# A two-layer convolution and state-space kernel: the first stage's 3×3 convolutions divided between TensorE and VectorE, with its normalising and copying on ScalarE

## The chip, the cores and the metric

The kernel runs on one core of one Trainium2 chip. The metric is the device time of one execution in microseconds (us). Of several executions the median counts. The profile is that of one further execution, and it carries its own time.

## What is computed

There are two layers over an image batch `x` of 4 images, 128 channels, 64×64 pixels, all in float32. The change lies in the first half of layer 0, which runs once for each image. Cut to that half, the reference is:

```python
x  = group_norm(x)                                  # 32 groups of 4 channels
feat = gelu(dwconv2d(x, conv1_w) + conv1_b)         # depthwise 3x3, 'SAME'
ca   = sigmoid(relu(feat.mean((2, 3)) @ ca1_w.T) @ ca2_w.T)
feat = gelu(dwconv2d(feat * ca, conv2_w) + conv2_b) # depthwise 3x3 again
scores = sigmoid(einsum('bchw,oc->bohw', feat, head_w) + head_b)
final  = 0.7 * scores + 0.3 * sigmoid(10 * var(x over channels))
idx    = argsort(-mean of final over 4x4 patches)   # 256 patches per image
x1  = x with its patches in the order idx, transposed to tokens, + pe
x1n = layer_norm(x1) * norm_g + norm_b
```

`x1n` goes through a Mamba-like block (projection, a scan over 4096 tokens, projection back). Layer 1 follows: a selective scan and a spectral convolution over the same 4 × 4096 tokens. None of that code is changed.

## The kernel before

`conv_attn_hybrid` calls four stages one after the other: `layer0_front` (the code above), `layer0_scan`, `spectral_weights` and `layer1`. `layer0_front` stores its result for each image with `dma_start(xnt[b], xn)` (L259), and `layer0_scan` starts from it. In `layer0_front` a scheduler orders each engine's instructions. It puts in the semaphore waits, also those of an engine for itself, and may interleave independent work. Each engine then executes its list strictly in that order. (`layer0_scan` and what follows have an order written out by hand.)

One image, `for b in range(NB)`, goes like this. Channels are on the 128 partitions.

1. **Group norm.** The image `xs` is loaded. Eight `bn_stats` (L111) and a `bn_aggr` on VectorE, two tiny matmuls (L119, L124) and a GpSimd power (L127) give mean and scale. VectorE writes the normalised image into `xg`, a 66×66 tile with a border of zeros (L129). The `bn_stats` of the next image are interleaved into this image's first convolution.
2. **Patches.** Four VectorE copies (L134) bring the image into patch order (`xp1`). TensorE transposes it to tokens in eight groups of four transposes (L149). For each group VectorE adds `pe` into `x1` (L151) and takes `bn_stats` of both (L153, L154). Per half image, 32 `bn_aggr` follow (L156, L157).
3. **Layer norm of the tokens.** VectorE makes `ve` (L160), GpSimd raises it to the power −0.5 (`r1`, L161), and 32 VectorE instructions subtract the mean and multiply by `r1`, in place in `x1` (L166).
4. **First convolution.** A depthwise 3×3 convolution as nine matmuls, one for each tap: the stationary matrix is diagonal (`d1`, the tap's weights on the diagonal), the moving one is a shifted window of `xg`. `conv` (L90 to L99) sums nine matmuls of 128×128 by 128×512 into one PSUM tile `ps`; eight such tiles cover an image. ScalarE takes each through Gelu into `f1` with a running sum (L176).
5. **Channel attention.** The sums become `mean` (L181, L182), two small matmuls and a Sigmoid give `ca` (L190), and VectorE scales the nine diagonals by it (`d2b`, L192).
6. **Second convolution.** The same on `f1` with `d2b`; Gelu into `f2` in patch order (L196).
7. **Ranking.** 32 small matmuls make the scores (`sc`, L206; the first 16 read the tiles 0 to 3 of `f2`, the next 16, in four groups of four, the tiles 4 to 7), then a short VectorE chain compares all patches and makes a permutation matrix `perm`.
8. **Reordering.** Eight PSUM tiles of four matmuls `x1 × perm` each (L255). VectorE evicts each with `* norm_g + norm_b` into `xn`, with a step of 16 elements between neighbours in the output (L258).

The pool `pm` has four PSUM tiles; transposes, convolutions and reordering share them. Each float32 matmul shows as two records in the trace, so an image's convolution has 8 × 9 × 2 = 144 of them.

Of the kernel before, what the change touches and what calls it, by code (L numbers as in the profile page):

```python
# [8 lines left out]
F32 = mybir.dt.float32  # L9
AF = mybir.ActivationFunctionType  # L10
ALU = mybir.AluOpType
# [3 lines left out]

NB = 4
L = 4096


@with_exitstack  # L20
def layer0_front(ctx: ExitStack, tc, ident, half, w, x, xnt, perm_t):
# [4 lines left out]
    nc = tc.nc  # L26
    cp = ctx.enter_context(tc.tile_pool(name="a_c", bufs=1))
    xp = ctx.enter_context(tc.tile_pool(name="a_x", bufs=1))
    sm = ctx.enter_context(tc.tile_pool(name="a_sm", bufs=2))
# [3 lines left out]
    def load(name, shape, src):  # L33
        t = cp.tile(shape, F32, name=name)
        nc.sync.dma_start(t, src)
        return t

    def column(name, src):
        return load(name, [src.shape[0], 1], src.unsqueeze(1))

    w1 = load("w1", [128, 9], w["conv1_w"])
    w2 = load("w2", [128, 9], w["conv2_w"])
    b1, b2 = column("b1", w["conv1_b"]), column("b2", w["conv2_b"])
# [3 lines left out]
    ng, nb = column("ng", w["norm_g"]), column("nb", w["norm_b"])  # L47
    pe = load("pe", [128, 2, 16, 128], w["pe"].rearrange("(h p) (o c) -> p h o c", p=128, o=16))


    d1 = cp.tile([128, 9, 128], F32, name="d1")
    d2 = cp.tile([128, 9, 128], F32, name="d2")
    for tap in range(9):
        nc.vector.tensor_scalar(d1[:, tap, :], ident, w1[:, tap : tap + 1], None, ALU.mult)
        nc.vector.tensor_scalar(d2[:, tap, :], ident, w2[:, tap : tap + 1], None, ALU.mult)

# [24 lines left out]
    def bordered(name):  # L81

        t = xp.tile([128, 66, 66], F32, tag=name, name=name)
        nc.vector.memset(t[:, 0, :], 0.0)
        nc.vector.memset(t[:, 65, :], 0.0)
        nc.vector.memset(t[:, 1:65, 0:1], 0.0)
        nc.vector.memset(t[:, 1:65, 65:66], 0.0)
        return t, t[:, 1:65, 1:65]

    def conv(img, diag, h, oy):  # L90

        ps = pm.tile([128, 8, 64], F32, tag="mm", name="conv")
        for tap in range(9):
            dy, dx = divmod(tap, 3)
            y0 = 32 * h + oy + dy
            nc.tensor.matmul(  # L96
                ps, diag[:, tap, :], img[:, y0 : y0 + 29 : 4, dx : dx + 64], start=tap == 0, stop=tap == 8
            )
        return ps  # L99

    def by_patch(t, oy):

        return t.rearrange("c (py px oy ox) -> c oy py px ox", px=16, oy=4, ox=4)[:, oy]

    for b in range(NB):

        xs = xp.tile([128, L], F32, tag="xs", name="xs")
        nc.sync.dma_start(xs, x[b])
# [19 lines left out]
        xg, inside = bordered("xg")  # L128
        nc.vector.tensor_scalar(  # L129
            inside, xs.rearrange("c (y x) -> c y x", x=64), gm, rs, ALU.subtract, ALU.mult  # L130
        )
        xp1 = xp.tile([128, L], F32, tag="patches", name="xp1")
        for oy in range(4):
            nc.vector.tensor_copy(  # L134
                by_patch(xp1, oy), inside[:, oy::4, :].rearrange("c py (px ox) -> c py px ox", ox=4)
            )


        x1 = xp.tile([128, 2, 16, 128], F32, tag="x1", name="x1")
# [3 lines left out]
        mv1 = sm.tile([128, 2, 16, 2], F32, tag="mv1", name="mv1")  # L143
        patches = xp1.rearrange("c (h p o) -> c h o p", h=2, o=16)
        for h in range(2):
# [12 lines left out]
        r1 = sm.tile([128, 2, 16], F32, tag="r1", name="r1")  # L158
# [2 lines left out]
        nc.gpsimd.tensor_tensor(  # L161
            r1.rearrange("p h o -> p (h o)"), ve.rearrange("p h o -> p (h o)"), half[:, :32], ALU.pow
        )
        for h in range(2):
            for o in range(16):
                nc.vector.tensor_scalar(  # L166
                    x1[:, h, o, :], x1[:, h, o, :], mv1[:, h, o, 0:1], r1[:, h, o : o + 1],
                    ALU.subtract, ALU.mult,
                )


        f1, inside1 = bordered("f1")
        sums = sm.tile([128, 8], F32, tag="sums", name="sums")
        for i in range(8):
            h, oy = divmod(i, 4)
            nc.scalar.activation(  # L176
                inside1[:, 32 * h + oy : 32 * h + oy + 29 : 4, :], conv(xg, d1, h, oy), AF.Gelu, bias=b1,
                accum_out=sums[:, i : i + 1],
            )
        mean = sm.tile([128, 1], F32, tag="mean", name="mean")  # L180
        nc.vector.tensor_reduce(mean, sums, AX, ALU.add)  # L181
        nc.vector.tensor_scalar(mean, mean, 1.0 / L, None, ALU.mult)  # L182
        hid = ps1.tile([32, 1], F32, tag="one", name="hid")
# [4 lines left out]
        nc.tensor.matmul(cap, ca2, hs, start=True, stop=True)  # L188
        ca = sm.tile([128, 1], F32, tag="ca", name="ca")
        nc.scalar.activation(ca, cap, AF.Sigmoid)  # L190
        d2b = xp.tile([128, 9, 128], F32, tag="d2b", name="d2b")
        nc.vector.tensor_scalar(d2b, d2, ca, None, ALU.mult)  # L192
        f2 = xp.tile([128, L], F32, tag="patches", name="f2")
        for i in range(8):
            h, oy = divmod(i, 4)
            nc.scalar.activation(  # L196
                by_patch(f2, oy)[:, 8 * h : 8 * h + 8],
                conv(f1, d2b, h, oy).rearrange("c py (px ox) -> c py px ox", ox=4), AF.Gelu, bias=b2,
            )


# [2 lines left out]
        for h in range(2):  # L204
            for o in range(16):
                nc.tensor.matmul(  # L206
                    sc[:, h, o : o + 1], fpatch[:, h, o, :], head,
                    start=True, stop=True,
# [38 lines left out]

        xn = xp.tile([128, 3 + L], F32, tag="xn", name="xn")
        nc.vector.memset(xn[:, 0:3], 0.0)
        ranked = xn[:, 3:].rearrange("c (r o) -> c o r", o=16)  # L250
        for o in range(0, 16, 2):
            ps = pm.tile([128, 2, 256], F32, tag="mm", name="ranked")
            for i in range(2):
                for h in range(2):
                    nc.tensor.matmul(  # L255
                        ps[:, i, :], x1[:, h, o + i, :], perm[:, h, :], start=h == 0, stop=h == 1
                    )
            nc.vector.tensor_scalar(ranked[:, o : o + 2, :], ps, ng, nb, ALU.mult, ALU.add)  # L258
        nc.sync.dma_start(xnt[b], xn)  # L259


# [6 lines left out]
def layer0_scan(ctx: ExitStack, tc, ident, w, x, xnt, perm_t, x2):  # L268
# [141 lines left out]
    def put_back(b, om):  # L410

        for h in range(2):
            xs = sm.tile([128, 8, 4, 64], F32, tag="xs", name="xs")
            cols = bass.ts(h, L // 2)
            nc.sync.dma_start(xs.rearrange("c py oy x -> c (py oy x)"), x[b][:, cols])
# [825 lines left out]
@with_exitstack  # L1241
def conv_attn_hybrid(ctx: ExitStack, tc, w, out):
    nc = tc.nc
    const = ctx.enter_context(tc.tile_pool(name="const", bufs=1))
    dram = ctx.enter_context(tc.tile_pool(name="dram", bufs=1, space=DRAM))
    ident = const.tile([128, 128], F32, name="ident")
    make_identity(nc, ident)
    half = const.tile([128, 32], F32, name="half")
    nc.vector.memset(half, -0.5)
    x2 = dram.tile([NB, 128, L], F32, name="x2")  # L1250
    x3 = dram.tile([NB, 128, L], F32, name="x3")
    x = w["x"]
    with tc.tile_pool(name="ordered", bufs=1) as pool:
        xnt = dram.tile([NB, 128, 3 + L], F32, name="xnt")
        perm_t = pool.tile([128, NB, 2, 256], F32, name="perm_t")
        layer0_front(tc, ident, half, w, x, xnt, perm_t)
        layer0_scan(tc, ident, w, x, xnt, perm_t, x2)
    pqd = dram.tile([NK, 2, 128, 4, 128], F32, name="pqd")
    mud = dram.tile([128, 4, 3, 128], F32, name="mud")
    spectral_weights(  # L1260
        tc, w["sigma"], w["M_u"], w["M_phi_plus"], w["M_phi_minus"], w["log_weights"], w["gumbel"], pqd, mud
    )
    layer1(
        tc, ident, half, w["W_in"], w["W_delta"], w["W_B"], w["W_C"], w["W_out"], w["A"], w["phi"], pqd, mud,
        x2, x3, out,
    )
# [48 lines left out]
```

## Time and profile before

| | |
|---|---|
| median of 3 runs | 22132.84 us (22130.33 to 22134.94) |
| the profiled execution | 22129.28 us, its span 22127.6 us |
| end of the first stage's last reordering (L258) in the span | 774.8 us |
| time from one image to the next in the first stage | 187.5 us |
| engine busy time in the span: TensorE, VectorE, ScalarE, GpSimd | 80%, 92%, 71%, 91% |

Engine names in the profile are PE (TensorE), PEld (its weight loads), DVE (VectorE), ACT (ScalarE), POOL (GpSimd) and SP (SyncE, which issues the DMAs). In a timeline or a chain, a row's first number is its start and its second its length, in us from the start of the span. A group's row gives busy time in us and the mean length of one instruction in ns, then the idle time of its engine just before it and what ended that. Consecutive instructions of VectorE or ScalarE overlap a little in the records, so the step from one start to the next is shorter than the length of one.

### The profile page before, as it was taken

What the parts mean: (1) busy time and instruction counts of PE and PEld (TensorE: products, weight loads), DVE (VectorE), ACT (ScalarE), POOL (GpSimd) and SP (SyncE); (2) the same over time, 40 slices, a digit from 0 to 9 for tenths busy, and PEclk for the clock granted to TensorE, in tenths of its full rate; (3) what the DMA queues carried; (4) which work ended last, traced back from release to release, by engine and by line L of the source; (5) the groups of instructions that cost most, each with busy time, mean ns of one, the idle gap of its engine ahead of it and who ended that gap; (6) DMA issues with size and microseconds to landing.
All of it is one profiled execution on the core that took longest, in us unless ns stands there. A gap on an engine that the chain in (4) does not pass through costs nothing.

```text
span 22127.6 us, 292872 instructions
## 1 busy us (share of the span) xinstructions
PE 17758.9 (80%) x99156; PEld 7777.4 (35%) x99156; DVE 20448.7 (92%) x11842; ACT 15725.0 (71%) x28971; POOL 20181.7 (91%) x5932
## 2 busy tenths in 40 slices
PE   8788844474867888886858888869598899999999
PEld 4444421131323333342323333324233344434344
DVE  3588879999999999999999999999999999999993
ACT  0477747777777777777777777777777777777773
POOL 0477759999999999999999999999999999999993
PEclk9899976686988999997979999979699999999999
DMA  0255544464656776675656777757577677777775
GB/s 27 78 139 140 140 136 151 150 198 151 206 186 200 218 222 218 218 220 180 213 173 217 220 219 218 220 179 229 164 225 222 216 233 233 232 230 230 230 226 154
DMA packets 2399971, 4238.15 MB, mean 192 GB/s; under 512 B 778200, under 2 KB 1235968, under 8 KB 2395136
## 3 DMA queue, kind: packets, MB, share of 16 engines
q1 hardware_dynamic: 2398464, 4219.40, 62.0%
q8 instruction: 781, 12.80, 0.2%
q14 instruction: 726, 5.95, 0.1%
HBM read 3600.52 MB, written 617.88 MB: 191 GB/s over the span
## 4 chain that ended last, share of the span: by engine, by line
DVE 49%; POOL 17%; PE 14%; ACT 9%; issue 6%; DMA 4%; SPq 0%; DVEq 0%; POOLq 0%; ACTq 0%
DVE s L1097 43%; POOL v L1085 16%; ACT da L1094 6%; PE conv L1045 6%; DVE states L493 3%; PE conv L96 2%; DMA yd<-ye 2%; PE yp L1114 2%; DVE p L497 2%; PE fin L989 1%; ACT f L485 1%; PE y L509 1%; PE mm L402 0%; ACT t L764 0%; ACT ye L1120 0%
## 5 line engine op out<-in xcount | busy, mean ns | idle before, releaser
L1085 POOL TENSOR_TENSOR v<-u,dlb 128x2044 f32<-128x2044 f32 x4096 | 18343.1, 4522 | 111.5 <-DMA dlb<-delta 93.7
L1097 DVE TENSOR_TENSOR_SCAN s<-da,v 128x1024 f32<-128x1024 f32 x8192 | 18056.5, 2270 | 383.3 <-ACT da L1094 315.7
L1094 ACT ACTIVATE da<-dlb,at 128x511 f32<-128x511 f32 x16384 | 11299.4, 690 | 2062.9 <-DVE s L1097 1598.3
L1045 PE MATMUL conv<-strip,tok 128*128 128x512 f32 (+3 forms) x20480 | 8646.5, 552 | 3.9 <-DMA strip<-in_phi 3.8
L1114 PE MATMUL yp<-s,c 128*32 128x256 f32 x65536 | 5015.4, 437 | 2972.2 <-DVE s L1097 1617.2
L1045 PEld LDWEIGHTS conv<-strip,tok 128*128 128x128 f32 x20480 | 3689.4, 192 | 4132.0 <-issue 3754.7
L1114 PEld LDWEIGHTS yp<-s,c 128*32 128x32 f32 x65536 | 1987.9, 121 | 6755.1 <-issue 1831.8
L1089 ACT COPY v<-vf 128x4 f32<-128x4 f32 x4096 | 813.4, 199 | 2260.8 <-DVE s L1097 2142.4
L471 POOL TENSOR_TENSOR v<-dx,bcb 128x1024 f32<-128x1024 f32 x512 | 1207.2, 2358 | 433.4 <-DVE states L493 427.9
L989 PE MATMUL fin<-conved,pq 128*128 128x512 f32 (+1 forms) x3200 | 1423.1, 540 | 13.5 <-ACT conved L1056 4.2
L493 DVE TENSOR_TENSOR_SCAN states<-f,v 128x1024 f32<-128x1024 f32 x512 | 1176.0, 2297 | 172.5 <-ACT f L485 123.3
L1120 ACT COPY ye<-yp 128x512 f32<-128x512 f32 x2048 | 1186.1, 579 | 148.9 <-DMA yd<-ye 132.2
L485 ACT ACTIVATE f<-dt,an 128x255 f32<-128x255 f32 x2048 | 973.4, 476 | 418.7 <-DVE states L493 368.0
L509 PE MATMUL y<-p,ident 128*128 128x512 f32 x2048 | 1005.1, 619 | 149.4 <-DVE p L497 144.4
L1056 ACT COPY conved<-conv 128x512 f32<-128x512 f32 x1344 | 778.2, 579 | 338.3 <-PE conv L1045 336.8
L497 DVE TENSOR_TENSOR p<-states,bcb 128x1024 f32<-128x1024 f32 x512 | 627.1, 1225 | 41.1 <-DVE states L493 2.7
L989 PEld LDWEIGHTS fin<-conved,pq 128*128 128x128 f32 x3200 | 532.0, 194 | 226.0 <-issue 164.1
L509 PEld LDWEIGHTS y<-p,ident 128*128 128x128 f32 x2048 | 368.4, 195 | 680.4 <-issue 355.2
L127 POOL TENSOR_TENSOR rs<-sq,half 128x1 f32<-128x1 f32 x4 | 2.2, 560 | 485.2 <-DVE sq L125 485.2
L402 PE MATMUL mm<-ow,yg 128*32 128x128 f32 x2048 | 283.2, 298 | 106.8 <-ACT om L406 105.3
L402 PEld LDWEIGHTS mm<-ow,yg 128*32 128x32 f32 x2048 | 236.8, 139 | 213.6 <-ACT om L406 128.4
L1005 DVE TENSOR_TENSOR xo<-xo,fin 128x512 f32<-128x512 f32 x32 | 21.3, 665 | 300.8 <-PE fin L997 300.8
(232 smaller groups left out, 6259.3 us busy)
## 6 DMA issues: line engine op xcount, KB each, us to landing
dlb<-delta SPq DMA_DIRECT2D x4096, 512.0 KB, 4.1
strip<-in_phi SPq DMA_DIRECT2D x1536, 448.0 KB, 4.7
yd<-ye SPq DMA_DIRECT2D x2048, 256.0 KB, 4.0
bcb<-bcd SPq DMA_DIRECT2D x1024, 256.0 KB, 4.2
strip<-in_phi SPq DMA_DIRECT2D x1024, 256.0 KB, 4.3
pq<-pqd SPq DMA_DIRECT2D x1088, 64.0 KB, 3.9
yt<-yd SPq DMA_DIRECT2D x4096, 4.0 KB, 3.3
pq<-pqd SPq DMA_DIRECT2D x256, 128.0 KB, 4.0
```

What stands on the lines that cost most here:

```text
L471: nc.gpsimd.tensor_tensor(v, ready[n][2][:, :, bass.ts(i, SUB)].unsqueeze(1).broadcast_to((128, 2, 2, SUB)), bc[:, 0].unsqueeze(2).broadca ...
L485: nc.scalar.activation(factors[j % 2][:, a, k, 1:], ready[n][1][:, k, SUB * i + 1 : SUB * i + SUB], AF.Exp, scale=an[:, k, 2 * g + a : 2 * ...
L493: nc.vector.tensor_tensor_scan(states.rearrange(flat), factors[j % 2].rearrange(flat), v.rearrange(flat), 0.0, ALU.mult, ALU.add)
L497: nc.vector.tensor_tensor(p, states, bc[:, 1].unsqueeze(2).broadcast_to((128, 2, 2, SUB)), ALU.mult)
L509: nc.tensor.matmul(t.rearrange("p k t -> p (k t)"), ident, p[:, a].rearrange("p k t -> p (k t)"), start=g == 0 and a == 0, stop=False, ski ...
L989: nc.tensor.matmul(fin[:, bass.ds(c0, w)], pq[:, n, :], u[:, bass.ds(c0, w)], start=begin and n == 0, stop=end and not partly, skip_group_ ...
L1045: nc.tensor.matmul(ps[:, skip:], tok[:, 1 - r if side else r, j, :], strip[:, bass.ds(c0 - lo, TS - skip)], start=src == sources[0] and j ...
L1085: nc.gpsimd.tensor_tensor(v[:, :, :, 1:], ready[0][:, :, 1:].unsqueeze(1).broadcast_to((128, VD, 2, TS - 1)), dl[:, :, 1:].unsqueeze(2).br ...
L1094: nc.scalar.activation(da[:, h, 1:], dl[:, d % VD, 1:], AF.Exp, scale=at[:, h, d : d + 1])
L1097: nc.vector.tensor_tensor_scan(s[:, d % GD].rearrange("p h t -> p (h t)"), da.rearrange("p h t -> p (h t)"), v[:, d % VD].rearrange("p h t ...
L1114: nc.tensor.matmul(yp[i // 2][bass.ts(q, 32), i % 2], c[:, h, t], s[:, :, h, t], start=h == 0, stop=h == 1)
L1120: nc.scalar.copy(ye, yp[j].rearrange("p i d t -> p i t d"))
```

## The change

`PT = 4` of the nine taps stay on TensorE. The other five are VectorE instructions `scalar_tensor_tensor`, each of which computes `window * weight + sum`. The first reads the PSUM tile as its `sum`; the others work in place on an SBUF tile `sum`, of which the pool has three. Gelu reads `sum` in place of PSUM. The weights of the second convolution's VectorE taps are scaled by `ca` too (`w2b`), and the diagonals are made for four taps only.

ScalarE takes over three things from VectorE: the four copies into patch order, the 32 normalising instructions (as `x * r1 + m1`, with a new small VectorE instruction that makes `m1 = -mean * r1`), and the eight evictions of the reordering.

```diff
-    d1 = cp.tile([128, 9, 128], F32, name="d1")
-    d2 = cp.tile([128, 9, 128], F32, name="d2")
-    for tap in range(9):
+    d1 = cp.tile([128, PT, 128], F32, name="d1")
+    d2 = cp.tile([128, PT, 128], F32, name="d2")
+    for tap in range(PT):
...
-    def conv(img, diag, h, oy):
+    def conv(img, diag, taps, h, oy):
         ps = pm.tile([128, 8, 64], F32, tag="mm", name="conv")
+        sum_ = sm.tile([128, 8, 64], F32, tag="conv", name="sum", bufs=3)
         for tap in range(9):
             dy, dx = divmod(tap, 3)
             y0 = 32 * h + oy + dy
-            nc.tensor.matmul(
-                ps, diag[:, tap, :], img[:, y0 : y0 + 29 : 4, dx : dx + 64], start=tap == 0, stop=tap == 8
-            )
-        return ps
+            rows = img[:, y0 : y0 + 29 : 4, dx : dx + 64]
+            if tap < PT:
+                nc.tensor.matmul(ps, diag[:, tap, :], rows, start=tap == 0, stop=tap == PT - 1)
+            else:
+                nc.vector.scalar_tensor_tensor(
+                    sum_, rows, taps[:, tap : tap + 1], ps if tap == PT else sum_, ALU.mult, ALU.add
+                )
+        return sum_
...
-            nc.vector.tensor_copy(
+            nc.scalar.copy(
                 by_patch(xp1, oy), inside[:, oy::4, :].rearrange("c py (px ox) -> c py px ox", ox=4)
...
+        m1 = sm.tile([128, 2, 16], F32, tag="m1", name="m1")
+        nc.vector.scalar_tensor_tensor(m1, mv1[:, :, :, 0], -1.0, r1, ALU.mult, ALU.mult)
         for h in range(2):
             for o in range(16):
-                nc.vector.tensor_scalar(
-                    x1[:, h, o, :], x1[:, h, o, :], mv1[:, h, o, 0:1], r1[:, h, o : o + 1],
-                    ALU.subtract, ALU.mult,
+                nc.scalar.activation(
+                    x1[:, h, o, :], x1[:, h, o, :], AF.Identity, bias=m1[:, h, o : o + 1],
+                    scale=r1[:, h, o : o + 1],
                 )
...
-        d2b = xp.tile([128, 9, 128], F32, tag="d2b", name="d2b")
+        d2b = xp.tile([128, PT, 128], F32, tag="d2b", name="d2b")
         nc.vector.tensor_scalar(d2b, d2, ca, None, ALU.mult)
+        w2b = sm.tile([128, 9], F32, tag="w2b", name="w2b")
+        nc.vector.tensor_scalar(w2b, w2, ca, None, ALU.mult)
...
-            nc.vector.tensor_scalar(ranked[:, o : o + 2, :], ps, ng, nb, ALU.mult, ALU.add)
+            nc.scalar.activation(ranked[:, o : o + 2, :], ps, AF.Identity, bias=nb, scale=ng)
```

The two calls of `conv` pass `w1` and `w2b` as `taps`.

More of the change, by code (lines that the diff above doesn't have):

```diff
@@ L17 @@
 L = 4096
+PT = 4
 @with_exitstack
@@ L176, in layer0_front @@
             nc.scalar.activation(
-                inside1[:, 32 * h + oy : 32 * h + oy + 29 : 4, :], conv(xg, d1, h, oy), AF.Gelu, bias=b1,
+                inside1[:, 32 * h + oy : 32 * h + oy + 29 : 4, :], conv(xg, d1, w1, h, oy), AF.Gelu, bias=b1,
                 accum_out=sums[:, i : i + 1],
@@ L197, in layer0_front @@
                 by_patch(f2, oy)[:, 8 * h : 8 * h + 8],
-                conv(f1, d2b, h, oy).rearrange("c py (px ox) -> c py px ox", ox=4), AF.Gelu, bias=b2,
+                conv(f1, d2b, w2b, h, oy).rearrange("c py (px ox) -> c py px ox", ox=4), AF.Gelu, bias=b2,
             )
```

## The prediction

> **What bounds the kernel now.** I first read where the span's end comes from. The page's chain for the whole span gives the first stage's convolution little:
>
> ```profile
> DVE s L1097 43%; POOL v L1085 16%; ACT da L1094 6%; PE conv L1045 6%; DVE states L493 3%; PE conv L96 2%; DMA yd<-ye 2%; PE yp L1114 2%; DVE p L497 2%; PE fin L989 1%; ACT f L485 1%; PE y L509 1%; PE mm L402 0%; ACT t L764 0%; ACT ye L1120 0%
> ```
>
> So L96 holds 2% of the end, and no more than that can be won there. But the stage stands alone in front of the rest, so each us it loses is a us of the span. Then the same chain for the second image (start, length, what):
>
> ```profile
> 210.62 1.13 DVE xn L258
> ...
> 231.26 64.44 PE conv L96 x144
> 295.72 0.78 ACT f L176 x2
> 296.52 1.28 ACT L190
> 298.02 0.83 DVE d2b L192
> 298.89 64.23 PE conv L96 x144
> 363.13 13.67 PE sc L206 x64
> ```
>
> The reader is to see that both convolutions lie on the chain for their full length: 8 × 64.3 = 515 us in all. Third, the busy times in these two stretches (length, then PE, PEld, DVE, ACT, POOL busy with counts, clock, DMA):
>
> ```profile
> 231.26:295.72 64.46, 64.43 (x144) 27.82 (x144) 22.27 (x103) 6.96 (x16) 5.44 (x1) 0.97 0.00 0
> 298.89:363.13 64.24, 64.24 (x146) 28.08 (x146) 0.00 (x0) 6.09 (x8) 0.00 (x0) 0.97 0.00 0
> ```
>
> TensorE is full, VectorE has 22 us of work in the first and none in the second. Last, the groups that price what moves (busy, mean ns, idle before):
>
> ```profile
> L161 POOL TENSOR_TENSOR r<-ve,half 128x32 f32<-128x32 f32 x4 | 21.8, 5442 | 108.7 <-DVE ve L160 108.7
> L166 DVE TENSOR_SCALAR x<-x,mv,r 128x128 f32<-128x128 f32 x128 | 33.2, 341 | 20.6 <-POOL r L161 20.6
> L151 DVE TENSOR_TENSOR x<-tp,pe 128x512 f32<-128x512 f32 x32 | 21.6, 675 | 0.0
> L111 DVE BATCH_NORM_STATS2 st<-xs 128x6 f32<-128x512 f32 x32 | 19.9, 679 | 11.9 <-DMA xs<-in_x 11.9
> L236 DVE SCALAR_TENSOR_TENSOR junk<-scores,score,before 128x256 f32<-128x256 f32 x8 | 3.8, 479 | 0.0
> L258 DVE TENSOR_SCALAR xn<-ranked,ng,nb 128x512 f32<-128x512 f32 x32 | 36.6, 1143 | 21.6 <-PE ranked L255 21.6
> L764 ACT ACTIVATE t<-t,ms,rs 128x128 f32<-128x128 f32 x256 | 105.4, 482 | 111.8 <-POOL ms L760 111.6
> ```
>
> L166 carries a wait to remember: VectorE idles 20.6 / 4 = 5.2 us an image for GpSimd's power. And the timeline of VectorE where the first convolution has just begun:
>
> ```profile
> 239.85 0.15 DVE L157 BATCH_NORM_AGGREGATE mv<-st 128x2 f32<-128x6 f32 x1
> 239.93 0.69 DVE L111 BATCH_NORM_STATS2 st<-xs 128x6 f32<-128x512 f32 x1
> 240.53 0.17 DVE L160 TENSOR_SCALAR ve<-mv 128x32 f32<-128x32 f32 x1
> ```
>
> VectorE is still at the token statistics until 239.93, 8.67 us after TensorE began (231.26).
>
> **What the Trainium skill says.** (1) "Vector Engine (DVE) Microarchitecture Reference", section 5.2, gives 1.0417 ns per column plus about 75 ns per instruction, and more for an output that hops every element. The trace agrees: L151 steps by 0.59 us for 512 columns, and L258, which writes with a step of 16, takes 1143 ns. (2) Section 7 of the same page says that this very instruction with two non-bf16 SBUF sources halves its throughput. The trace disagrees: L236 has two float32 SBUF sources and takes 479 ns for 256 columns, less than the 533 ns that half rate needs for the columns alone. The measurement decides. (3) "ScalarE: Activation LUTs", "Table sets: the hidden batching unit", has copy and identity in every set, so the moved work brings no table loads of its own; the built program adds none but one at the very start. (4) "TensorE: Matmul & The Clock Gate", Part 1: after an idle window of about 3.4 us TensorE runs at half clock until it has been busy for one. The trace agrees: near 301 us the second convolution's records step by 0.86 us, later by 0.433.
>
> **The change part by part, per image.**
>
> Price of a VectorE tap. L236 steps by 0.41 us (its timeline), 0.14 above its 256 columns; 512 columns give 0.53 + 0.14 = 0.67 us from start to start. A tap that needs the one right before it waits for its end: L236's 0.479 less 0.267 for its columns plus 0.53 gives 0.745, plus 0.04 (gaps between dependent rows such as L121 and L122), 0.785. Bounds: 0.60 (L151's step, without the pointer) and 1.20 (half rate, 1.07 + 0.13). I take 0.67 and 0.785.
>
> First convolution. TensorE needs 64 records × 0.433 = 27.7 us, no longer the limit. VectorE is. In the built program its order after the last aggregate is: first tap of tile 0, `ve`, first tap of tile 1, then `m1`, which waits for GpSimd's power. Behind `m1` stand the other 38 taps: the 5.2 us wait, which before held up only L166, now holds up the convolution. Counted from 239.93: `ve` ends at 0.83, the power at 0.91 + 5.44 = 6.35, `m1`, and on at 6.5. Eight taps of tiles 0 and 1 alternate: 5.3, to 11.8. Tile 2 alternates with the next image's statistics: 5 × 0.67 + 8 × 0.60 + 0.4 = 8.5, to 20.3. Tiles 3 and 4 need `sum` buffers that Gelu 0 and 1 free. ScalarE's order puts all 32 normalisations before Gelu 0: from 6.65, 31 × 0.39 (four L764 rows take 1.65 us) + 0.48 to 19.2, table load 1.28, Gelu 0.7: 21.25. So VectorE stalls 1 us; the second buffer comes at 22.0. Tiles 3 and 4 end at 28.0, tiles 5 and 6 (10 × 0.67) at 34.7, tile 7 alone (4 × 0.785 + 0.745) at 38.55. Gelu and `mean` follow after 0.81 as before: 39.35. From TensorE's start that is 8.67 + 39.35 = 48.0 us, where before it was 64.44 + 0.81 = 65.25. Gain 17.2.
>
> Attention. `d2b` shrinks from 1152 to 512 columns; 820 ns less 640 × 0.52 (L129's 2415 ns over 4096 columns, less the fixed part) is 0.49. Gain 0.33. `w2b` runs beside TensorE: nothing.
>
> Second convolution. TensorE: 27.7 plus 1.9 for the cold start (64.24 − 144 × 0.433) = 29.6. VectorE starts when tile 0 is done, near 5, and takes 3.9 a tile for the first three, then about 3.55, since the built order slips another tile's first tap between two: it ends near 35, Gelu at 35.7. But TensorE goes on with the scores: 16 matmuls (6.8 us) that read only tiles 0 to 3, to 36.4, and tile 7 is needed by the last four alone, at 41.5. The tail is hidden with 5 us to spare. Gain 64.24 − 29.6 = 34.6. Without that cover 6 us would come back.
>
> Copies to patch order. ScalarE's first is done later than VectorE's (an estimate of 1.04 us from "ScalarE: Activation LUTs", "What ACT_TABLE_LOAD costs": 186 ns + 0.833 per column; L134 takes 0.69), but VectorE no longer does four (2.50) before its first L151. First copy, 0.15, four transposes 0.95: L151 starts at 2.25 in place of 2.4. Gain 0.15.
>
> Evictions. They leave VectorE, so the next image's `gm` (L120) need not follow the last L258: gain 0.8, three times. On ScalarE one may take 0.69 (L341, step 1) to 2.3 (twice L258). TensorE brings a tile every 1.73; I take about 1.2, hidden. Above 1.73 each costs 8 × the excess. The 18 diagonals made at the start lie under the load of `xs`, which ends at 18.2: nothing.
>
> Sum: 4 × (17.2 + 34.6 + 0.33 + 0.15) + 3 × 0.8 = 209.1 + 2.4 = 211.5. Against the profiled execution 22129.3 − 211.5 = 21917.8; the median of the runs shown is 3.6 higher (22132.84), so 21921.
>
> **The rivals.** *Dependent taps do not alternate so well*: all at 0.785, 34 exposed taps × 0.12 = 4 us an image, the second convolution still covered: 21937. Nothing speaks strongly against it, as no row shows two chains alternating. *The stall is smaller*, by VectorE taking 0.60 a tap and ScalarE freeing buffers in time: up to 6 us an image, 21897. Against it: the power's 5442 ns is measured and stands in the order. *Half rate for taps with two SBUF sources*: first convolution 30 × 0.53 = 16 more, the second ends at 49.5, 8 past its cover: 24 × 4 = 96, 22017. L236 speaks against it. *TensorE stays at half clock in the second convolution*: 64 × 0.86 = 55, 25 × 4 = 100 more, 22021; against it, its stream has no gaps, as PSUM has four tiles of slack. *Slower than before*: the tap's price alone. With p us a tap, the first convolution costs 48.0 + 38 (p − 0.67) and the second to the end of the scores about 7.4 + 40 p, against 65.25 + 64.24 + 13.67 = 143.2 before; equal at p = 1.45. At 1.6 it would be 12 us an image slower, about 22180. No VectorE row of 512 columns with unit steps comes near that.
>
> **How the numbers follow.** My forecast with its own small errors 0.62; dependent taps 0.15; smaller stall 0.13; half rate 0.04; cold clock 0.04; slower 0.02. The first three span about 21885 to 21975 when the unknown eviction (up to 0.57 × 8 × 4 = 18) and another cold window (1.5 × 4 = 6) are added to the slower of them; that holds nine tenths less misjudged sums, about 0.8. A measurement of this kernel tells 0.2% (44 us) from no change; all cases but the last are faster by more: 0.97 faster, 0.01 same, 0.02 slower.
>
> **What would show it.** Right: 64 records of L96's kind per convolution; taps near 0.745 long; VectorE idle about 5 us in each first convolution, ended by GpSimd; the first lasting near 48 us and the second near 30, with no TensorE gap before the scores. Wrong: taps over 1 us, TensorE waiting in the second convolution or before the scores, evictions over 1.7 us.

## The result, and the profile after

| | before | after |
|---|---|---|
| median | 22131.58 us of 4 runs (22129.56 to 22134.94) | 21922.86 us of 4 runs (21919.48 to 21925.42) |
| span of the profiled execution | 22127.6 us | 21920.9 us |
| first load of the second stage is issued (`xin`) | 784.60 us | 578.41 us |
| the rest of the span | 21343.0 us | 21342.5 us |

The ratio is 0.9905, with a 95% interval of 0.9888 to 0.9923. The span is 206.7 us shorter, and 206.2 us of that are gone before the second stage issues its first load. The rest of the kernel takes the time it took. The forecast was 21921.

Line numbers have moved: L103 is now the convolution's matmul, L105 a tap on VectorE, L143 the copy into patch order, L174 `m1`, L177 the normalisation, L187 and L209 the two Gelus, L203 `d2b`, L219 the scores, L268 and L271 the reordering and its eviction.

This is the chain of waits of the kernel after, for its fourth image (start, length, what):

```profile
466.03 12.43 ACT x L177 x32
478.47 1.28 ACT L187
479.77 1.53 ACT f L187 x4
481.32 4.79 DVE sum L105 x8
...
486.63 6.11 DVE sum L105 x10
...
500.41 0.50 DVE d2b L203
500.95 30.95 PE conv L103 x64
531.90 13.66 PE sc L219 x64
```

Before, both convolutions stood in the chain as one TensorE row each (64.44 and 64.23 us in the second image). Now the first is a chain through ScalarE (the normalisations, a table load, the first Gelus) and then through VectorE's taps. TensorE has left it. The second is still a TensorE row, of 64 records in place of 144, and the scores follow without a gap. Next, the busy times in the two convolutions of the second image (start and end, length, then PE, PEld, DVE, ACT, POOL busy with counts, clock, DMA):

```profile
179.81:228.08 48.27, 31.16 (x64) 13.20 (x64) 41.83 (x118) 20.41 (x51) 5.44 (x1) 0.85 0.00 0
230.00:259.74 29.74, 29.74 (x65) 13.08 (x66) 23.45 (x34) 5.62 (x7) 0.00 (x0) 0.93 0.00 1
```

In the first, VectorE is busy for 41.83 of 48.27 us and TensorE for 31.16. In the second TensorE is full. The groups that price what moved (busy, mean ns of one, idle time before and what ended it):

```profile
L105 DVE SCALAR_TENSOR_TENSOR sum<-f,w2b,sum 128x512 f32<-128x512 f32 x128 | 94.4, 750 | 3.1
L105 DVE SCALAR_TENSOR_TENSOR sum<-xg,w,sum 128x512 f32<-128x512 f32 x128 | 88.5, 745 | 0.7
L177 ACT ACTIVATE x<-x,m,r 128x128 f32<-128x128 f32 x128 | 49.7, 480 | 25.4 <-DVE m L174 25.4
L271 ACT ACTIVATE xn<-ranked,nb,ng 128x512 f32<-128x512 f32 x32 | 39.0, 1218 | 52.3 <-PE ranked L268 52.3
L143 ACT COPY xp<-xg 128x1024 f32<-128x1024 f32 x16 | 15.8, 1057 | 36.7 <-DVE xg L138 36.7
```

A tap takes about 750 ns with two SBUF sources, and 739 to 743 ns where one source is in PSUM (the groups `sum<-xg,w,conv` and `sum<-f,w2b,conv` of L105). The halved rate that the Trainium skill gives for two such sources ("Vector Engine (DVE) Microarchitecture Reference", section 7) would need 1067 ns for the columns alone, so it does not hold for these float32 tiles. Last, the timeline of VectorE and ScalarE in the second image's first convolution, where TensorE begins at 179.81:

```profile
188.49 0.70 DVE L105 SCALAR_TENSOR_TENSOR sum<-xg,w,conv 128x512 f32<-128x512 f32 x1
194.83 0.19 DVE L174 SCALAR_TENSOR_TENSOR m<-mv,r 128x32 f32<-128x32 f32 x1 [4.90 <-POOL r L170]
194.94 5.38 DVE L105 SCALAR_TENSOR_TENSOR sum<-xg,w,sum 128x512 f32<-128x512 f32 x8
195.06 12.43 ACT L177 ACTIVATE x<-x,m,r 128x128 f32<-128x128 f32 x32 [6.30 <-DVE m L174]
200.24 0.74 DVE L105 SCALAR_TENSOR_TENSOR sum<-xg,w,conv 128x512 f32<-128x512 f32 x1
...
209.66 1.45 DVE L105 SCALAR_TENSOR_TENSOR sum<-xg,w,conv 128x512 f32<-128x512 f32 x2 [0.85 <-ACT f L187]
...
223.72 3.12 DVE L105 SCALAR_TENSOR_TENSOR sum<-xg,w,sum 128x512 f32<-128x512 f32 x4
227.72 0.16 DVE L192 TENSOR_REDUCE mean<-sums 128x1 f32<-128x8 f32 x1 [0.36 <-ACT f L187]
```

The reader is to see the two waits of VectorE, and that they belong together. `m1` waits 4.90 us for GpSimd's power, with all later taps behind it. The same `m1` releases ScalarE's 32 normalisations, which stand ahead of Gelu 0 on that engine, and Gelu 0 frees the `sum` buffer that tile 3 waits for at 209.66. Between the two, VectorE fills its time with tile 2 and the next image's statistics.

### The profile page after: what moved, and what is told of

The parts are those of the page before. It is cut to its first block, busy times and chain, and to the rows that moved or that the text cites. A ratio compares the mean times of both kernels' runs of the same rounds, so it can differ in the third digit from the quotient of the medians.

```text
span 21920.9 us, 291965 instructions
## 1 busy us (share of the span) xinstructions
PE 17505.8 (80%) x98516; PEld 7675.8 (35%) x98516; DVE 20589.4 (94%) x11984; ACT 15831.5 (72%) x29148; POOL 20181.2 (92%) x5932
## 3 DMA queue, kind: packets, MB, share of 16 engines
q14 instruction: 728, 5.96, 0.1%
## 4 chain that ended last, share of the span: by engine, by line
DVE 50%; POOL 17%; PE 11%; ACT 9%; issue 7%; DMA 3%; SPq 0%; DVEq 0%; POOLq 0%; ACTq 0%
DVE s L1110 43%; POOL v L1098 17%; ACT da L1107 6%; PE conv L1058 5%; DVE states L506 3%; DMA yd<-ye 2%; PE yp L1127 2%; DVE p L510 1%; PE fin L1002 1%; ACT f L498 1%; PE y L522 1%; PE mm L415 1%; ACT t L777 0%; ACT ye L1133 0%; ACT xz L362 0%
```

## The experiments

The theory to be tested is that of the prediction: after the last aggregate VectorE's own list sets the first convolution (the wait for the power, taps at 0.67 us, the wait for `sum` buffers, a tail of dependent taps), while TensorE's 64 records set the second, with VectorE's tail hidden under the scores. The rivals were that the wait for the power is what the stage really pays, so that it is worth its 5 us once removed; that ScalarE is what limits, through the buffers; and that part of the gain comes from the instructions given to ScalarE and not from the taps.

Each kernel is judged by two numbers. One is its time. The other is the moment at which the second stage's first load is issued, since only the stage ahead of it was edited. What lies after it was the same code in all kernels and took between 21341.0 and 21355.9 us, so a difference of 10 us between two spans says little, while the moment says it. A time given without the word median is that of one execution, the profiled one. "Mean" below is the time from the last aggregate to `mean` in the second image: 39.2 us in the kernel after.

**ScalarE's part alone.** All nine taps of both convolutions stay on TensorE. Copies, normalisations and evictions are on ScalarE as in the change.

```diff
-PT = 4
+PT = 9
...
-        return sum_
+        return ps
```

> All nine taps stay on TensorE; only the copies, normalisations and evictions go to ScalarE. My reading of the profiles (they save nothing on the chain but 0.87 us at three of the image starts and 0.1 us of the copies): 3 us less than the kernel before, about 22127. Rival (44 us of VectorE work an image of statistics, copies, normalisation and evictions is what the stage pays for, so taking a third of it away is worth something by itself): 10 us less or more.

The time was 22127.6 us, and the median 22136.2 for the kernel before on the same chip (7 runs, 22130.1 to 22142.7). The second stage began at 784.56 us (784.60 before). ScalarE's part alone is worth nothing at the end of the stage. The 32 normalisations had lain beside TensorE's 64 us. The rest of the zero is a sum: the next images' `gm` came 0.96 us earlier three times, as expected, and TensorE's clock took as much back. The four reorderings lasted 16.6 to 16.9 us in place of 15.3 to 15.5, since more of each ran at half clock (5.48 us of the third, 2.61 before), and the first convolutions took 1.0 us more together, while two of the second convolutions lost no time to it (62.57 us in place of 64.24). How the clock bears on these stretches is worked out in the next section.

**The taps alone.** Copies, normalisations and evictions go back to VectorE. The edit of the normalisations:

```diff
-                nc.scalar.activation(
-                    x1[:, h, o, :], x1[:, h, o, :], AF.Identity, bias=m1[:, h, o : o + 1],
-                    scale=r1[:, h, o : o + 1],
-                )
+                nc.vector.tensor_scalar(
+                    x1[:, h, o, :], x1[:, h, o, :], mv1[:, h, o, 0:1], r1[:, h, o : o + 1],
+                    ALU.subtract, ALU.mult,
+                )
```

> The taps are divided as in the changed kernel, but copies, normalisations and evictions stay on VectorE. In the built order the 32 normalisations stand, with the wait for the power in front, behind the second tap: 32 x 0.26 = 8.3 us more on VectorE in the first convolution, while the statistics of the next image partly move behind the taps. mean at about 44 us after the last aggregate in place of 39.2, attention 1 us longer, 0.87 us lost at three image starts: 22 to 26 us more than the changed kernel, about 21946. Rival (ScalarE moves are worth only their own 3 us): 21926.

The time was 21948.9 us, near what was expected, but only 16.0 of the 26 us were lost in the edited stage (594.42 against 578.41). The rest of this execution was 10 us longer too, so the agreement is partly chance. In VectorE's timeline the 32 normalisations stand between the wait and the taps, which go on at 208.00:

```profile
199.78 8.30 DVE L175 TENSOR_SCALAR x<-x,mv,r 128x128 f32<-128x128 f32 x32 [4.91 <-POOL r L170]
```

Of these 8.3 us only 2.9 came out at `mean` (42.1 us). VectorE no longer waits for a Gelu at tile 3, since ScalarE has no normalisations ahead of it, and half of the next image's statistics now stand behind `mean`, where they lengthen the time from `mean` to `d2b` from 1.73 to 3.20 us. So the taps bring nine tenths of the gain (190 of 206 us in the stage), and ScalarE's part is worth 16 us once the taps are there, though nothing without them.

**The wait for the power taken from VectorE.** GpSimd, which makes the power, multiplies `m1` itself.

```diff
-        nc.vector.scalar_tensor_tensor(m1, mv1[:, :, :, 0], -1.0, r1, ALU.mult, ALU.mult)
+        ms = sm.tile([128, 2, 16], F32, tag="ms", name="ms")
+        nc.vector.tensor_scalar(ms, mv1[:, :, :, 0], -1.0, None, ALU.mult)
+        nc.gpsimd.tensor_tensor(
+            m1.rearrange("p h o -> p (h o)"), ms.rearrange("p h o -> p (h o)"), r1.rearrange("p h o -> p (h o)"), ALU.mult
+        )
```

> m1 is made by GpSimd, so VectorE no longer waits for the power in the first convolution. Theory A (two waits in series: the power, then the sum buffers that the Gelus behind 32 normalisations free): the 4.9 us wait vanishes, VectorE reaches the fourth tile 5 us earlier and waits there about 6 us for Gelu, so the time stays within 2 us of the changed kernel (21922). Theory B (the power wait is a cost of its own): 4 x 4.9 = 20 us less, about 21903.

The time was 21931.5 us, and the stage ended 5.6 us later than after the change. The timeline of the second image says why:

```profile
191.12 5.96 POOL L170 TENSOR_TENSOR r<-ve,half 128x32 f32<-128x32 f32 x1 [27.23 <-DVE ms L175]
197.16 1.35 POOL L176 TENSOR_TENSOR m<-ms,r 128x32 f32<-128x32 f32 x1
198.54 12.42 ACT L181 ACTIVATE x<-x,m,r 128x128 f32<-128x128 f32 x32 [8.03 <-POOL m L176]
213.13 1.45 DVE L105 SCALAR_TENSOR_TENSOR sum<-xg,w,conv 128x512 f32<-128x512 f32 x2 [7.57 <-ACT f L191]
```

The 4.90 us wait has gone, and a wait of 7.57 us for a Gelu stands at tile 3. The path through ScalarE is as long as the one through VectorE. It even begins later here, as the multiplication takes GpSimd 1.35 us in this run (VectorE 0.19) and the power 5.96 (5.44 in the kernel after). The wait for the power is not worth its 5 us by itself.

**The other wait: six `sum` buffers in place of three.**

```diff
-        sum_ = sm.tile([128, 8, 64], F32, tag="conv", name="sum", bufs=3)
+        sum_ = sm.tile([128, 8, 64], F32, tag="conv", name="sum", bufs=6)
```

> Six sum buffers in place of three; the power wait stays. Theory A: no wait for Gelu any more, and the scheduler also puts the next image's statistics behind the taps: mean comes at 6.5 + 38 x 0.667 + about 1.5 = 33.3 us after the last aggregate in place of 39.3, the attention becomes about 1 us longer by the statistics; 5 us an image, about 20 us less, 21902. Rival C (VectorE is simply full with 40 taps and 8 statistics): at most the 0.85 us wait for Gelu, 3 us less.

The time was 21904.5 us and the stage 22.1 us shorter: `mean` fell from 39.2 to 32.8 us. Yet the trace of the kernel after shows only 0.85 us of waiting for these buffers. The statistics of the next image explain it. In the kernel after they lie among tile 2's taps and fill what would be a longer wait. With six buffers the taps go on (tiles 2 and 3 start at 194.83 in this run, right after tiles 0 and 1), and the statistics move to the end. There they lengthen the attention from 1.73 to 3.16 us, because they stand between its small instructions on VectorE.

**Both waits together.** The two edits above in one kernel.

> Both waits removed. Theory A: taps run from the last aggregate on, 40 x 0.667 = 26.7 us, with a remaining wait of 1 to 2 us for Gelu 0 at the seventh tile: mean at 29.7 us, about 8.5 us an image less the change, 35 us in all, 21888: more than the two single edits together (0 + 20). Theory B: 20 + 3 us less, 21900. Rival C: 3 us less.

It missed: 21907.7 us. The stage gained another 3.6 us over six buffers alone, and the rest of this execution was 6.9 us longer. Where the missing part of the stage is, one row shows:

```profile
205.81 0.75 DVE L105 SCALAR_TENSOR_TENSOR sum<-xg,w,conv 128x512 f32<-128x512 f32 x1 [3.48 <-ACT f L191]
```

Even six buffers run out at tile 6 when VectorE no longer waits for the power, since the first Gelu still stands behind 32 normalisations.

**The normalisations late.** Nothing needs the normalised tokens before the reordering. `m1` and its 32 instructions are written behind the loop of the second convolution.

```diff
-        m1 = sm.tile([128, 2, 16], F32, tag="m1", name="m1")
-        nc.vector.scalar_tensor_tensor(m1, mv1[:, :, :, 0], -1.0, r1, ALU.mult, ALU.mult)
-        for h in range(2):
...
+        m1 = sm.tile([128, 2, 16], F32, tag="m1", name="m1")
+        nc.vector.scalar_tensor_tensor(m1, mv1[:, :, :, 0], -1.0, r1, ALU.mult, ALU.mult)
+        for h in range(2):
...
         sc = ps1.tile([128, 2, 16], F32, tag="one", name="sc")
```

> m1 and the 32 normalisations are written behind the second convolution, so the scheduler fits them between the Gelus. m1 stands behind 11 taps, 7.7 us after the last aggregate, when the power (6.4) is done; three sum buffers stay. Theory A: no wait for the power, little for Gelu; mean at about 30.2 us in place of 39.3, attention 1 us longer: 8 us an image, 25 to 35 us in all, 21887 to 21897. Theory B: 20 us less. Rival C: 3 us less.

The time was 21893.2 us, the stage 37.6 us shorter, and `mean` came at 30.1 us. The timeline shows both waits gone with three buffers only:

```profile
181.85 5.38 DVE L105 SCALAR_TENSOR_TENSOR sum<-xg,w,sum 128x512 f32<-128x512 f32 x8
187.15 0.74 DVE L105 SCALAR_TENSOR_TENSOR sum<-xg,w,conv 128x512 f32<-128x512 f32 x1
187.81 0.18 DVE L208 SCALAR_TENSOR_TENSOR m<-mv,r 128x32 f32<-128x32 f32 x1
...
188.03 3.57 ACT L211 ACTIVATE x<-x,m,r 128x128 f32<-128x128 f32 x9
193.34 2.79 ACT L211 ACTIVATE x<-x,m,r 128x128 f32<-128x128 f32 x7
```

The scheduler has moved `m1` back up, but only to behind the power's end, and it puts the normalisations between the Gelus in groups. So `mean` comes 9.1 us earlier. Of this, 5.75 us are the two waits themselves; most of the rest is statistics, of which three of eight now stand behind `mean` (the time from `mean` to `d2b` is 2.61 us in place of 1.73). None of the three edits before brought that.

**How the taps are divided.** With two taps on TensorE in place of four:

```diff
-PT = 4
+PT = 2
```

> PT = 2: seven of nine taps on VectorE in both convolutions. By the price of 0.667 us a tap on the path: the first convolution 16 more taps, 10 us longer (the wait for Gelu shrinks by 0.85); the second is bound by VectorE now (tile 0 at 3.7, 56 taps to 43.9, Gelu, four scores: 46.3 in place of 43.4), 2.7 us longer. 12.7 us an image, 51 us in all: about 21974. If VectorE's work in the first convolution were not what sets its length, the first would stay as it is: 21933.

The time was 21967.6 us, the stage 35.0 us longer. `mean` came at 48.3 us: 16 more taps cost 9.05 us, less than 16 × 0.67 = 10.7. The second convolution was hardly longer (0.5 us from `d2b` to the comparison of the scores), but here VectorE's tail is no longer hidden. Some of TensorE's rows among the scores:

```profile
278.56 1.89 PE L219 MATMUL sc<-head,f 128*128 128x1 f32 x8 [4.07 <-ACT f L209]
287.82 1.89 PE L219 MATMUL sc<-head,f 128*128 128x1 f32 x8 [4.07 <-ACT f L209]
```

The score matmuls wait for Gelu, which waits for VectorE's taps. In the kernel after none of them waits. Four taps are thus near the balance in the second convolution: with four TensorE sets its end, with two VectorE.

**Five taps on TensorE in the first convolution, three in the second,** with the normalisations late and `m1` on GpSimd:

```diff
-PT = 4
+PT1, PT2 = 5, 3
```

> The normalisations are written behind the second convolution, m1 is GpSimd's, and TensorE takes five taps of the first convolution and three of the second. By the prices so far: first convolution bound by TensorE (36.5 us, then four taps of the last tile and Gelu: mean 31.7 us after the last aggregate in place of 39.2); second bound by VectorE (tile 0 at 4.5, 48 taps at 0.68 to 37.2, Gelu 0.75, the last four scores 1.7: scores end at 39.7 in place of 43.4). 11.2 us an image, 45 us in all: about 21877. If the second convolution's tail were hidden only for other reasons than the order of the scores, the stretch from d2b to s1 would grow, not shrink by 3.7 us.

The median was 21890.14 us of 4 runs (ratio to before 0.9888, 0.9872 to 0.9905), above what was expected by 13 us. The stage was 39.5 us shorter than after the change. The second convolution gained 2.8 us of 3.7 expected, and `mean` came at 32.9 us, later than with four taps (30.1). The rest of this execution was 13.4 us longer than in the kernel after.

**Four and three, and five and three, with `m1` on VectorE.** These two were run to tell whether the fifth tap was at fault, or GpSimd.

> The late normalisation with four taps on TensorE in the first convolution and three in the second. If the two gains add, the first convolution is that of the kernel that only normalises late (mean 30.0 us after the last aggregate) and the stretch from d2b to the comparison of the scores is that of the 5/3 split (41.7 us, 2.8 shorter than with four taps): 4 x 2.8 = 11 us below 21893, about 21882. If VectorE's extra tap in the second convolution comes out behind the scores, that stretch stays near 44.5 and the time at 21893 or above.

> The same with five taps on TensorE in the first convolution. Theory one: with the wait gone, TensorE sets the first convolution (80 records of 0.433 us are 34.6, 26.0 after the last aggregate, then the last tile's four taps 3.1 and Gelu 0.8: mean near 29.9), so it equals the run with four taps, about 21882. Theory two: VectorE still sets it, and eight taps fewer are worth 8 x 0.67 = 5.4 us an image, 21 in all: about 21861.

With four and three the median was 21874.35 us (21868.35 to 21881.7, 4 runs; ratio 0.9884, 0.9867 to 0.99), the fastest kernel here. The stage was 52.7 us shorter than after the change, and 15.1 us shorter than with the late normalisation alone, of which 14.5 us, over the four images, lie between `d2b` and the comparison of the scores. With five and three it was 21888.81 us (21880.27 to 21894.87), and neither theory held: `mean` came at 34.0 us, 4.1 us later than with four taps (29.9). Two causes can be told apart. In the run of five and three with `m1` on GpSimd, where VectorE does not wait for the power, the first tap of the last tile waits for TensorE:

```profile
206.59 0.75 DVE L106 SCALAR_TENSOR_TENSOR sum<-xg,w,conv 128x512 f32<-128x512 f32 x1 [1.21 <-PE conv L104]
```

TensorE's 80 records took 37.4 us in both runs with five taps. The expectation had 34.6, for it left out the half clock, at which TensorE spent 5.2 us of them. So theory one had the mechanism right and the length too short: 3.0 of the 4.1 us are TensorE's longer row (`mean` at 32.9 on GpSimd). The other 1.1 us go with the wait for the power. Four taps, with `m1` on VectorE:

```profile
182.84 0.74 DVE L106 SCALAR_TENSOR_TENSOR sum<-xg,w,conv 128x512 f32<-128x512 f32 x1
...
183.50 0.19 DVE L209 SCALAR_TENSOR_TENSOR m<-mv,r 128x32 f32<-128x32 f32 x1
```

Five taps, with `m1` on VectorE:

```profile
178.62 0.75 DVE L106 SCALAR_TENSOR_TENSOR sum<-xg,w,sum 128x512 f32<-128x512 f32 x1
...
184.70 0.19 DVE L209 SCALAR_TENSOR_TENSOR m<-mv,r 128x32 f32<-128x32 f32 x1 [5.33 <-POOL r L171]
184.81 0.74 DVE L106 SCALAR_TENSOR_TENSOR sum<-xg,w,conv 128x512 f32<-128x512 f32 x1
```

With five taps `m1` stands ahead of tile 1's first tap in VectorE's list, and the wait of 5.33 us is back with the later taps behind it. With four it stands behind tile 2's first tap, when the power is long done. Tile 1 is ready later with five taps (ten records a tile in place of eight), which may be why the scheduler saw room there. That reading was not tested. The place in the program's text does not settle the place in the engine's list.

## Why the prediction was right

Its sum for the stage was 211.5 us, and 206.2 were measured. The profiled execution was to take 21917.8 us and took 21922.63. That the median came within 2 us of the forecast is partly luck: 3.6 us were added for the distance between profiled execution and median, and in the kernel after there is none (21922.63 and 21922.86).

Step by step, for the second image (us):

| step | predicted | measured |
|---|---|---|
| from one tap to the next; if it needs the one before | 0.67; 0.785 | 0.66 (5.30 / 8); 0.78 |
| last aggregate done, after TensorE's start | 8.67 | 8.68 |
| taps go on after `m1`, after the aggregate | 6.5 | 6.45 |
| tiles 0 and 1 done | 11.8 | 11.75 |
| Gelu 0 has freed a buffer, tile 3 begins | 21.25 | 21.17 |
| tiles 3 and 4 done; 5 and 6 done | 28.0; 34.7 | 27.84; 34.45 |
| `mean` | 39.35 | 39.23 |
| second convolution on TensorE | 29.6 | 29.9; 29.65, 30.7 and 30.95 in the others |
| one eviction | about 1.2 | 1.22 |
| gain of the copies | 0.15 | 0.09 |
| gain of the attention, from `mean` to TensorE's start | 0.33 | 0.09 |
| gain at the next image's `gm` | 0.8 | 0.96 |
| reordering on TensorE | as before (15.3 to 15.5) | 15.35; 16.90, 15.77 and 15.88 in the others |

- **The price of a tap** held, and with it the rejection of half rate. It came from L236, a row of half the columns in another part of the stage. The bounds that were kept for it (0.60 and 1.20) were not needed.
- **The first convolution** held to 0.25 us in each of its stations. The step that decided was to read the built order and not the diff: `m1` stands ahead of 38 taps. The run with the late normalisations shows that the waits and what they drag along do cost 9.1 us at `mean`.
- **The second convolution** held in the first two images and lasted 1.1 and 1.35 us too long in the third and fourth (30.95 us in the chain above). The cause is its cold start, below.
- **The tail's cover** held. The last Gelu ends at 265.79. The scores run from 259.74 without a gap, and the last four of their 32 matmuls begin near 271.7 (28/32 of 13.66 us): 5.9 us to spare, and 5.8 in the prediction (41.5 less 35.7).
- **The attention** gained 0.09 us in place of 0.33. `d2b` did shrink (0.82 to 0.49 us). What was left out is that TensorE, no longer the bound, now idles before the attention's small matmuls. The timeline of the kernel after, and its busy times from 228 to 230 us, where the third number from the end is the clock:

```profile
228.12 0.26 PE L195 MATMUL hid<-mean,ca 128*32 128x1 f32 x2 [12.45 <-DVE mean L193]
...
228.62 0.58 PE L199 MATMUL cap<-hs,ca 32*128 32x1 f32 x2 [0.24 <-DVE hs L197]
```

```profile
228.00:230.00 2.00, 0.86 (x5) 0.69 (x5) 0.77 (x4) 1.16 (x2) 0.00 (x0) 0.50 0.00 0
```

Before, TensorE had idled 1.25 us there, the clock was 1.00 and `cap` took 0.38 us (`hid` 0.22). `w2b`, costed at nothing, does run beside TensorE.
- **TensorE's clock** is the term that was mis-sized. The prediction allowed one cold start of 1.9 us in the second convolution, the same for every image, and nothing in the attention and the reordering. The first image's reordering in two parts, after and then before:

```profile
143.21:148.68 5.47, 5.47 (x15) 4.36 (x15) 0.76 (x2) 1.21 (x1) 0.00 (x0) 0.50 0.00 0
148.68:160.11 11.43, 11.43 (x55) 10.07 (x53) 0.00 (x0) 7.32 (x6) 0.00 (x0) 1.00 0.00 0
```

```profile
195.27:197.53 2.26, 2.26 (x8) 1.79 (x8) 0.76 (x2) 0.00 (x0) 0.00 (x0) 0.50 0.00 0
197.53:210.58 13.05, 13.05 (x63) 11.52 (x61) 8.03 (x7) 0.00 (x0) 0.00 (x0) 1.00 0.00 0
```

Take half of the time at half clock (0.50) away, and the same length is left: 16.90 − 2.74 = 14.16 us after, 15.31 − 1.13 = 14.18 before. In the traces of all twelve kernels here the 48 reorderings come to 14.16 to 14.18 us in this way. The second convolutions of the kernel after spent 3.50, 4.03, 5.69 and 6.14 us at half clock, and 27.9 us is left of each. So the reorderings' loss is the clock's and not the evictions': ScalarE's 1.22 us do stay hidden. Why the clock comes back sooner in one image than in another was not tried.
- **The `gm` gain** held (0.96 us three times). **The copies** gained 0.09 us. Their line in the prediction doesn't add up: 1.04 + 0.15 + 0.95 is 2.14 us and not 2.25, which would have been a gain of 0.26.

The sum was too high by 5.3 us: 2.7 in the second convolutions, 2.1 in the reorderings and 1.0 in the attention, all three TensorE's clock in the main, and 0.3 because the last eviction of an image ends later on ScalarE (1.24 us after TensorE, 1.17 before). The first convolutions, the stage's start and the ways from one image to the next came out 0.8 us better. These are differences between the two kernels' timelines, image by image.

Of the rivals, *dependent taps* is excluded by the steps of 0.66 us, *half rate* by the 745 ns, *half clock* for the whole second convolution by its 29.65 to 30.95 us, and *slower than before* with the tap's price. *The smaller stall* is excluded for this order of instructions. As a limit it was too small, for the late normalisations gained more an image than its "up to 6 us".

## What to carry to other kernels

When work is taken off the engine that sets the end, price the new engine in its built order: one short instruction that waits for another engine holds up everything queued behind it, and what it releases elsewhere may come back as the next wait. Where two waits start from the same event, look for one edit that removes both. Here moving the event's consumer behind the urgent work shortened the stage by 37.6 us, more buffers alone by 22.1, and buffers together with another engine for `m1` by 25.7. A wait of 0.85 us in the trace can hide more than it shows where a scheduler has filled it with other work, so look at what stands in front of it as well. And price the relieved engine again too: TensorE, now idle for longer, did its next work in part at half clock.

## What the runs showed of the hardware

- TensorE's time at half clock (0.50 in the traces) costs half of itself: 48 reorderings of 15.3 to 17.0 us all come to 14.16 to 14.18 us once half of that time is taken away.
- Small tensor_tensor instructions on GpSimd are dear, and their price is not constant. A multiplication of 128×32 float32 took 1.35 us in two kernels and 0.25 to 0.84 us in a third (five and three taps, `m1` on GpSimd), against 0.19 on VectorE for `m1`. The power next to it took 5.44 us in most runs and up to 5.97 in others. Taps on VectorE meanwhile are not the cause: with the late normalisations they ran beside it and it took 5.44 us, and with five and three taps and `m1` on VectorE it took 5.91 us while VectorE stood still. The cause stays open.
- An eviction on ScalarE with a step of 16 float32 elements between its outputs took 1218 ns for 512 columns, and one with unit steps 0.67 us (L341 of the kernel before). The first also reads a scale for each partition, and no run changed the step alone, so the step's share is not shown.
- The same code after the first stage took 21341.0 us in one profiled execution and 21355.9 in another, and the median of the kernel before moved between 22129.68 and 22136.22 us from one comparison to the next. What causes this was not found. For an edit in one stage the moment at which that stage ends is the better measure.
